# An LSTM step's input and forget gates moved to PSUM, its output gate to an activation of its own, around a re-timed TensorE queue

## The chip, the cores and the metric

The kernel runs on one core of a Trainium2 chip. The metric is the device time of one execution in microseconds. A profile of one further execution is shown beside it; its durations are used for all working.

## The reference

An LSTM over 1024 steps with batch 2 and 256 hidden units is added to its input, and a mixture-of-experts layer over the 2048 resulting tokens is added to that. Cut to what matters:

```
def step(carry, xw_t):
    prev_h, prev_c = carry
    a = xw_t + prev_h @ Wh                      # (2, 1024): i, f, o, g
    i, f, o = sigmoid(a[:, :H]), sigmoid(a[:, H:2*H]), sigmoid(a[:, 2*H:3*H])
    g = tanh(a[:, 3*H:])
    next_c = f * prev_c + i * g
    next_h = o * tanh(next_c)
    return (next_h, next_c), next_h
x = x + lstm(x, cond, Wx, Wh, b)
x = x + moe(x, cond, ...)      # 2 shared experts (silu, 512 wide), 8 routed (gelu, 256 wide), top 2
```

All is float32. The steps of the LSTM depend on each other; the expert layer of a token needs only that token's h.

## The kernel before, in words

The program is one long unrolled stream. `for t in range(T)` walks the 1024 steps. Hidden units lie in K = 2 chunks m of 128. A step goes through these instructions, for m = 0 and then m = 1:

- TensorE (all its instructions are issued by the helper `product`, L255): 32 products `ps<-wh_sb,h`, in the order of `BLOCKS`: three blocks need only chunk 0 of h, then come those that need chunk 1. Float32 makes two passes of each product, so 64 matmuls and 64 weight loads. They add onto the input projections, which small products with `inputs` (`inject`) have put into the bank of these gates before. Chunk m = 0 of the gates is complete after the fifth block.
- VectorE: `transpose(m)` (L787) turns the gates in PSUM so that a gate's values stand beside each other.
- ScalarE: `squash(m)`: one sigmoid of i, o and f together (L790, six values a partition) and one tanh of g (L791), both from PSUM to the SBUF tile `results`.
- VectorE: `forget(m)`, f * c (L794; c is read in PSUM); `cell(m)`: a small copy `seen` (L798), which holds VectorE's queue until g's tanh is there, and a scan of four values (L799), which forms i * g + f * c, writes c to the PSUM bank `cells[m]`, and reads i, g and f * c in SBUF.
- ScalarE: `squash_cell(m)`, tanh(c) (L807), PSUM to PSUM.
- VectorE: `output(m)`, h = o * tanh(c) (L810), into the SBUF tile that the next step's products read.

VectorE's queue order in a step is: transpose 0, transpose 1, forget 0, seen 0, scan 0, forget 1, seen 1, scan 1, output 0, output 1, then at most one or two pieces of filler.

Beside this chain the class `Fill` deals out the rest of the work: input projections for the next 128 steps and the expert layer of a finished group of steps (`GROUPS`), in units, a few after each step: `run_pe` after the 32 products, `run` for ScalarE, `run_dve(0.6)` for VectorE (estimated microseconds that a step may take). `PACES` says in how many steps a group's units have to be spread. A unit that opens one of two PSUM banks waits until VectorE work has let one go. A step without units may get a filler product `busy` with the identity matrix, but only if the first step of its eight had no units either (`spare`). After this come the `inject` products of the next eight steps' bank; their number is chosen with the list `WAITS` so that a boundary of 256 TensorE instructions (`FETCH`) does not fall on the first 16 of the next step's products (`EARLY`). The last group (32 steps) and what is left of the one before it are worked off after the last step (`drain`).

Of the kernel before, what the change touches and what calls it, by code (L numbers as in the profile page):

```python
# [9 lines left out]
F32 = mybir.dt.float32  # L10
BF16 = mybir.dt.bfloat16
AF = mybir.ActivationFunctionType
ALU = mybir.AluOpType
# [3 lines left out]
P = 128  # L17
N = 2
T = 1024
D = 256  # L20
K = D // P
Q = 4
ROWS = P // Q
PAIR = ROWS // 2
TH = PAIR // N
TB = 2 * TH
XB = 128
LOAD = 2
E = 8
# [3 lines left out]
TOP_K = 2  # L33
LAST = 32

GROUPS = [128] * 3 + [32] + [128] * 4 + [64, LAST]

PACES = [128] * 7 + [56, 31, 0]
FILL_BANKS = 2


# [1 line left out]
ROOM = 4  # L43
# [3 lines left out]


FETCH = 256
EARLY = 16  # L50
WAITS = (
    1, 8, 16, 24, 32, 40, 48, 56, 64, 72, 80, 88, 96, 104, 112, 120, 128, 136, 144, 149,
    152, 157, 160, 160, 165, 168, 176, 181, 184, 189, 192, 197, 200, 208, 216, 224, 232,
    240, 248, 256, 264, 272, 280, 288, 296, 304, 312, 320, 328, 336, 344, 352, 360, 368,
    376, 384, 392, 400, 408, 416, 419, 421, 423, 424, 428, 430, 432, 435, 437, 439, 440,
    440, 447, 448, 456, 464, 472, 480, 488, 496, 504, 512, 520, 528, 529, 536, 544, 552,
    560, 568, 576, 584, 592, 600, 608, 616, 624, 632, 640, 648, 656, 664, 672, 680, 688,
    688, 696, 704, 712, 720, 728, 736, 744, 752, 760, 768, 776, 784, 792, 800, 808, 816,
    824, 832, 840, 848, 856, 864, 872, 880, 888, 896, 904, 912, 920, 928, 930, 933, 935,
    936, 940, 942, 944, 947, 949, 951, 952, 956, 958, 960, 963, 965, 968, 976, 984, 992,  # L60
    999, 1000, 1004, 1006, 1008, 1011, 1013,
)
ISSUED = -188
OUT_SCALE = 1.0 / (NS + TOP_K)
# [9 lines left out]
class Fill:  # L74
# [36 lines left out]
    def run(self, queue, budget):  # L111
        while queue and queue[0][0] <= self.step and queue[0][1] <= budget:
            _, cost, fn = queue.popleft()
            budget -= cost
            fn()

    def run_pe(self, count, room):
        done = 0
# [16 lines left out]
def lstm_moe_kernel(  # L135
# [16 lines left out]
    nc = tc.nc  # L152
# [63 lines left out]
    for t0 in range(2 * XB, T, XB):  # L216
        for k in range(K):
            cols = slice(t0, t0 + XB)
# [32 lines left out]
    fill = Fill()  # L251

    def product(*operands, **how):
        fill.issued += 4
        nc.tensor.matmul(*operands, **how)  # L255

    def bank():
        if fill.last:
            pool, name = behind[0]
            behind.rotate(-1)  # L260
        else:
            pool, name = fill_ps, "ps_f"
        return pool.tile([P, 2, 256], F32, name=name)
# [22 lines left out]
    def experts(t0, S):  # L286
# [215 lines left out]
        def last_shared_down(c):  # L502
            if c < 0:
                st["down"] = bank()
                x_kqj = st["down"][:W, 0, :].rearrange("p (q k j) -> p k q j", q=Q, k=K)
                for k in range(K):
                    product(
                        x_kqj[:, k], mov[k], ident_s,
                        start=(k == 0), stop=False, skip_group_check=True,
                    )  # L510
                return
            ps, n = st["down"], NS * HS // P
            for g in range(2):
                product(
                    ps[g * W : (g + 1) * W, 0, :], st["h_s"][:, c + g, :W], w2_sb[:, c + g, :],
                    start=(c + g == 1), stop=(c + 2 == n), skip_group_check=True,
                )
            if c + 2 == n:
                fill.to_dve(0.45, lambda: begin_sum(0, ps), lag=0)
# [11 lines left out]

        def last_add(e2, ps):
            acc = st["acc", 0]
            nc.vector.scalar_tensor_tensor(  # L534
                acc, ps[:, 0, :], st["gates"][:, e2 : e2 + 1], acc, ALU.mult, ALU.add
            )
            fill.let_go()
            if e2 == E // 2 - 1:
                both = bank()[:W, 0, :]
                product(both, fold, acc, start=True, stop=True)  # L540
                total = work.tile([P, D], F32, name="y")[:W]
                nc.scalar.activation(total, both, AF.Copy)  # L542
                nc.sync.dma_start(out=out_tn[t0 : t0 + S], in_=total)

        ups = [
            (int(j == 0), W // P if W > P else 1, lambda b=b, j=j: up(b, j))
# [45 lines left out]
    def h_cols(t):  # L592
        at = EDGE + t % TB * ROWS
        return hs[t // TB % 2][:, :, at : at + N]
# [59 lines left out]
    def inject(banks, grp, i, pieces=1):  # L654
        m, q = divmod(i, Q)
        blk, g = divmod(grp, XB // TH)
        assert all((blk, 4 * m + 2 * (q // 2) + c, g * PAIR) in made for c in range(2))
        for piece in range(pieces):
            w0, w1 = 64 * piece // pieces, 64 * (piece + 1) // pieces
            product(  # L660
                banks[m][0][q * ROWS : (q + 1) * ROWS, w0:w1],
                pairs(blk)[:, 2 * m + q // 2, g].rearrange("p c r -> p (c r)"),
                ident[:, q % 2 * 64 + w0 : q % 2 * 64 + w1],
                start=(piece == 0), stop=False, skip_group_check=True,
            )
# [21 lines left out]

    def results():
        flat = stepsp.tile([P, TB, K, 8 * N], F32, name="results")
        sgm = flat[:, :, :, : 6 * N].rearrange("p u m (a n z) -> p u m a n z", n=N, z=2)
        gf = flat[:, :, :, 6 * N :].rearrange("p u m (n z) -> p u m n z", z=2)
        for m in range(K):
            nc.scalar.activation(sgm[:, :, m, 0, :, 0], zero[:, :, m], AF.Copy)
        return sgm, gf


    nc.scalar.activation(stepp.tile([P, N], F32, name="seen0"), zero[:, 0, 0], AF.Sigmoid)
    nxt_results = results()

    cells = [cells_ps.tile([P, 3, N, 2], F32, name=f"c{m}") for m in range(K)]
    c_prev = [cells[m][:, 1] for m in range(K)]
    for m in range(K):
        nc.vector.memset(cells[m], 0.0)
    nc.vector.tensor_copy(h_cols(0), cond_sb)
# [19 lines left out]
    for t in range(T):  # L728
        fill.step = t
        grp, u = divmod(t, TB)  # L730
        if t % TH == 0:
            cur, nxt = nxt, [gates_tile(m) for m in range(K)]
            ps, turned, busy = [a[0] for a in cur], [a[1] for a in cur], nxt[0][2]
            spare = False
        if u == 0:
            sgm, gf = nxt_results
        if t == 1:
            queue_inputs(0, ROWS)
        if t == XB // 2:
# [15 lines left out]
                    skip_group_check=True,  # L755
                )
        left = max(1, due - t)
        done = fill.run_pe(-(-len(fill.pe) // left), ROOM)
        if t % TH == 0:
            spare = not done  # L760
        if spare and not done:
            product(
                busy, ident, ident.unsqueeze(1).to_broadcast([P, 2, P]),
                start=(t % TH == 0), stop=False, skip_group_check=True,
            )

        if t // TH + 1 < T // TH:
            put = put if t % TH else 0
            fill.issued += WAITS.count(t)

            left = K * Q - put
            count = next(
                (n for n in range(max(0, t % TH + 1 - put), left + 1)
                 if -(fill.issued + 4 * n) % FETCH > EARLY), left)
            first = -(fill.issued + 4 * count) % FETCH
            for i in range(count):
                more = i == count - 1 and first <= EARLY
                inject(nxt, t // TH + 1, put, 2 + first // 4 if more else 1)
                put += 1

        rows = slice(N * (t % TH), N * (t % TH + 1))
        gates = [turned[m].rearrange("p (a r) -> p a r", r=PAIR)[:, :, rows] for m in range(K)]
        c_new = [cells[m][:, t % 2] for m in range(K)]
        seen = [stepp.tile([P, N], F32, name=f"seen{m}") for m in range(K)]

        def transpose(m):
            nc.vector.transpose(turned[m], ps[m])  # L787

        def squash(m):
            nc.scalar.activation(sgm[:, u, m, :, :, 1], gates[m][:, 0:3], AF.Sigmoid)  # L790
            nc.scalar.activation(gf[:, u, m, :, 0], gates[m][:, 3], AF.Tanh)  # L791

        def forget(m):
            nc.vector.tensor_mul(gf[:, u, m, :, 1], sgm[:, u, m, 2, :, 1], c_prev[m][:, :, 1])  # L794

        def cell(m):

            nc.vector.tensor_copy(seen[m], gf[:, u, m, :, 0])  # L798
            nc.vector.tensor_tensor_scan(  # L799
                c_new[m].rearrange("p n z -> p (n z)"),  # L800
                sgm[:, u, m, 0].rearrange("p n z -> p (n z)"),
                gf[:, u, m].rearrange("p n z -> p (n z)"),
                0.0, ALU.mult, ALU.add,
            )

        def squash_cell(m):
            nc.scalar.activation(cells[m][:, 2, :, 0], c_new[m][:, :, 1], AF.Tanh)  # L807

        def output(m):
            nc.vector.tensor_mul(h_cols(t + 1)[:, m], sgm[:, u, m, 1, :, 1], cells[m][:, 2, :, 0])  # L810

        for fn in (transpose, squash):
            for m in range(K):
# [4 lines left out]
            squash_cell(m)  # L818
        for m in range(K):
            output(m)  # L820
        if u == TB // 2 and t + TB < T:
            nxt_results = results()
        else:
            fill.run(fill.act, 1.0)
        c_prev = c_new
        if rest and t % LOAD == 0:
            load_next()
        if t == 2 * TB:
# [3 lines left out]
        if (t + 1) % XB == 0 and t + 1 + XB < T:  # L832
            queue_inputs((t + 1) // XB + 1)
        if u < TB - 1:
            fill.run_dve(0.6)
            continue
        if t < T - 1:
            residual(grp, int(grp == 0 or t - TB in ends), TB)
# [89 lines left out]
```

## Time and profile before

| what | value |
|---|---|
| median of 3 runs | 2257.78 us (2252.64 to 2258.61) |
| the profiled execution | 2256.97 us, of which the span is 2254.8 us |
| busy in the span | PE 2033.5, weight loads 1484.8, DVE 1571.3, ACT 909.5 us |
| mean granted TensorE clock | 0.996 |
| first transposition starts / last pair starts | 10.2 us / 2232.4 us into the span |

The span is the time from the first to the last instruction of the program. Busy time counts the union of an engine's instructions; a group's line gives line, engine, operation, output<-inputs, shape and count, then busy time and mean ns of one, then idle time of the engine just before and what ended it. The `results`, `c` and `ps` of the names stand for all buffers of that name.

### The profile page before, as it was taken

Reading aid. Unit: us, or ns where it says so; the run is one execution under the profiler, and the core shown is the slowest. Engines: PE = TensorE matmul, PEld = TensorE weight load, DVE = VectorE, ACT = ScalarE, POOL = GpSimd, SP = SyncE. Lnnn points to the kernel's source line nnn. Section 1 sums busy time; section 2 is a strip of 40 time slices with the busy share of each in tenths; the row PEclk is TensorE's granted clock in tenths of the full one; section 3 lists DMA queues with packets and bytes.
Section 4 is the critical chain, followed back from the end, with each engine's and each line's share of the span. In section 5 each row is a group of like instructions: output and inputs, shape, how many; then the busy total and the mean of one; then the engine's idle time right before and its main releaser. Section 6 shows DMA issues by size and latency. Waiting matters only on the chain.

```text
span 2254.8 us, 159246 instructions
## 1 busy us (share of the span) xinstructions
PE 2033.5 (90%) x70612; PEld 1484.8 (66%) x70612; DVE 1571.3 (70%) x11041; ACT 909.5 (40%) x6487; POOL 2.7 (0%) x9
## 2 busy tenths in 40 slices
PE   8988899888989889998798899988898988989998
PEld 6666666666666666777666666666666666667787
DVE  5666667776777667777667767676676776667776
ACT  3334344433444334443344443444434344334443
POOL 0000000000000000000000000000000000000000
PEclk9999999999999999999999999999999999999999
DMA  2111100000000000000000000000000000000000
GB/s 65 35 35 35 35 28 5 5 5 7 7 5 5 5 7 7 5 7 7 5 6 5 5 5 7 7 4 5 5 7 7 4 5 5 7 7 5 5 9 7
DMA packets 15330, 23.84 MB, mean 11 GB/s; under 512 B 2864, under 2 KB 14128, under 8 KB 14640
## 3 DMA queue, kind: packets, MB, share of 16 engines
q1 hardware_dynamic: 14352, 12.62, 1.9%
q8 instruction: 552, 9.04, 1.7%
q14 instruction: 138, 1.13, 0.2%
q10 hardware_dynamic: 288, 1.05, 0.1%
HBM read 11.56 MB, written 2.10 MB: 6 GB/s over the span
## 4 chain that ended last, share of the span: by engine, by line
PE 61%; DVE 36%; issue 3%; DMA 0%; SPq 0%; ACT 0%
PE ps L255 53%; DVE ps L787 10%; DVE c L799 10%; PE ps_f L255 8%; DVE results L794 7%; DVE seen L798 6%; DVE h L810 3%; DMA wh_sb<-in_wh_dram 0%; SPq L165 0%; DVE acc L534 0%; SPq L173 0%; SPq L171 0%; SPq L170 0%; DVE acc L492 0%; ACT y L542 0%
## 5 line engine op out<-in xcount | busy, mean ns | idle before, releaser
L255 PE MATMUL ps<-wh_sb,h 128*32 128x64 f32 x65536 | 1143.8, 221 | 214.3 <-DVE h L810 210.5
L255 PEld LDWEIGHTS ps<-wh_sb,h 128*32 128x32 f32 x65536 | 975.1, 110 | 393.1 <-DVE h L810 386.8
L787 DVE STREAM_TRANSPOSE ps<-ps 128x64 f32<-128x64 f32 x2048 | 543.4, 265 | 498.5 <-PE ps L255 426.0
L790 ACT ACTIVATE results<-ps 128x6 f32<-128x6 f32 x2048 | 361.3, 176 | 1103.8 <-DVE ps L787 1009.4
L810 DVE TENSOR_TENSOR h<-results,c 128x2 f32<-128x2 f32 x2048 | 314.2, 153 | 168.4 <-ACT c L807 168.2
L807 ACT ACTIVATE c<-c 128x2 f32<-128x2 f32 x2048 | 321.5, 157 | 217.5 <-DVE c L799 181.7
L799 DVE TENSOR_TENSOR_SCAN c<-results 128x4 f32<-128x4 f32 x2048 | 358.2, 175 | 0.0
L791 ACT ACTIVATE results<-ps 128x2 f32<-128x2 f32 x2048 | 342.4, 167 | 0.0
L798 DVE COPY seen<-results 128x2 f32<-128x2 f32 x2048 | 332.8, 162 | 0.0
L794 DVE TENSOR_TENSOR results<-results,c 128x2 f32<-128x2 f32 x2048 | 319.3, 156 | 0.0
L255 PEld LDWEIGHTS ps<-ident,inputs 128*32 128x32 f32 x2090 | 124.0, 108 | 265.7 <-issue 228.4
L255 PE MATMUL ps<-ident,inputs 128*32 128x64 f32 (+2 forms) x2090 | 263.9, 230 | 0.3
L255 PE MATMUL ps_f<-x2T,w_sb 128*128 128x256 f32 (+3 forms) x640 | 173.4, 379 | 0.0
L255 PE MATMUL ps_f<-x2T,r_sb 128*128 128x256 f32 (+3 forms) x640 | 173.2, 378 | 0.0
L255 PE MATMUL ps_f<-r_sb,h_r 128*128 128x256 f32 (+1 forms) x520 | 165.9, 419 | 0.9 <-DVE acc L492 0.9
L255 PEld LDWEIGHTS ps_f<-x2T,r_sb 128*128 128x128 f32 (+1 forms) x640 | 88.5, 184 | 22.8
L255 PEld LDWEIGHTS ps_f<-x2T,w_sb 128*128 128x128 f32 (+1 forms) x640 | 86.7, 184 | 21.8 <-issue 0.2
L255 PEld LDWEIGHTS ps_f<-r_sb,h_r 128*128 128x128 f32 (+1 forms) x520 | 80.0, 184 | 23.3 <-DVE acc L492 1.3
L255 PE MATMUL ps_f<-xT_sb,wx_sb 128*128 128x256 f32 (+2 forms) x384 | 84.5, 346 | 0.3 <-ACT inputs L613 0.3
L255 PE MATMUL ps<-ident 128*128 128x256 f32 x232 | 82.8, 443 | 1.4 <-POOL ident masks.py:199 1.4
L255 PE MATMUL ps_f<-w_sb,h_s 128*128 128x256 f32 (+1 forms) x256 | 82.6, 419 | 0.0
L492 DVE SCALAR_TENSOR_TENSOR acc<-ps_f,gate,acc 128x256 f32<-128x256 f32 (+1 forms) x128 | 61.1, 478 | 1.2 <-PE ps_f L255 1.0
(87 smaller groups left out, 475.1 us busy)
## 6 DMA issues: line engine op xcount, KB each, us to landing
r_sb<-in_r_w1T_dram SPq DMA_DIRECT2D x16, 128.0 KB, 2.5
r_sb<-in_r_w2T_dram SPq DMA_DIRECT2D x16, 128.0 KB, 2.1
out_dram<-acc SPq DMA_DIRECT2D x15, 128.0 KB, 2.1
xT_sb<-in_xT_dram SPq DMA_DIRECT2D x14, 128.0 KB, 2.5
wx_sb<-in_wx_dram ACTq DMA_DIRECT2D x2, 512.0 KB, 4.3
wh_sb<-in_wh_dram SPq DMA_DIRECT2D x2, 512.0 KB, 6.2
w_sb<-in_s_w1T_dram SPq DMA_DIRECT2D x8, 128.0 KB, 2.2
w_sb<-in_s_w3T_dram SPq DMA_DIRECT2D x8, 128.0 KB, 2.2
```

Of the source, the lines that this page charges most:

```text
L255: nc.tensor.matmul(*operands, **how)
L492: nc.vector.scalar_tensor_tensor(acc, ps, st["gate"][:, i, e : e + 1], acc, ALU.mult, ALU.add)
L787: nc.vector.transpose(turned[m], ps[m])
L790: nc.scalar.activation(sgm[:, u, m, :, :, 1], gates[m][:, 0:3], AF.Sigmoid)
L791: nc.scalar.activation(gf[:, u, m, :, 0], gates[m][:, 3], AF.Tanh)
L794: nc.vector.tensor_mul(gf[:, u, m, :, 1], sgm[:, u, m, 2, :, 1], c_prev[m][:, :, 1])
L798: nc.vector.tensor_copy(seen[m], gf[:, u, m, :, 0])
L799: nc.vector.tensor_tensor_scan(c_new[m].rearrange("p n z -> p (n z)"), sgm[:, u, m, 0].rearrange("p n z -> p (n z)"), gf[:, u, m].rearrang ...
L807: nc.scalar.activation(cells[m][:, 2, :, 0], c_new[m][:, :, 1], AF.Tanh)
L810: nc.vector.tensor_mul(h_cols(t + 1)[:, m], sgm[:, u, m, 1, :, 1], cells[m][:, 2, :, 0])
```

## The change

Four things change together.

1. The step's cell. The sigmoid takes i and f alone (four values) and writes them to `cells[m]`, the PSUM bank that holds c; o's sigmoid becomes an activation of its own, put ahead of tanh(c) in ScalarE's queue, and goes to SBUF. The scan reads i in PSUM. f * c reads f in PSUM and c in a copy in SBUF, which a new `tensor_copy` makes behind each `output(m)`. The small instruction `seen` becomes a product that reads the PSUM bank and g. The zeroing activations of `results()` go.
2. The TensorE queue. The order after the 32 products becomes: a product that opens the bank of eight steps (always on their first step, 32 columns wide if units follow, 2 x 128 columns otherwise), injections, units, and the filler product in every step that has neither units nor that opening product. The rule for the number of injections counts what follows them (`then`), has new limits, and a new list `WAITS`.
3. The groups: steps 800 to 927 become two groups of 64, `PACES` are set anew, and `run_dve` gets 0.55 in place of 0.6.
4. The end: the last sum and its way out are cut into two halves of 128 columns.

```diff
-GROUPS = [128] * 3 + [32] + [128] * 4 + [64, LAST]
-PACES = [128] * 7 + [56, 31, 0]
+GROUPS = [128] * 3 + [32] + [128] * 3 + [64] * 3 + [LAST]
+PACES = [128] * 6 + [60, 60, 48, 27, 0]
...
-EARLY = 16
+EARLY = 12
...
         def last_add(e2, ps):
             acc = st["acc", 0]
-            nc.vector.scalar_tensor_tensor(
-                acc, ps[:, 0, :], st["gates"][:, e2 : e2 + 1], acc, ALU.mult, ALU.add
-            )
+            if e2 < E // 2 - 1:
+                cols = [slice(0, D)]
+            else:
+                cols = [slice(0, P), slice(P, D)]
+                total = work.tile([P, D], F32, name="y")[:W]
+            for i, c in enumerate(cols):
+                nc.vector.scalar_tensor_tensor(
+                    acc[:, c], ps[:, 0, c], st["gates"][:, e2 : e2 + 1], acc[:, c],
+                    ALU.mult, ALU.add,
+                )
+                if len(cols) > 1:
+                    both = bank()[:W, 0, :P]
+                    product(both, fold, acc[:, c], start=True, stop=True)
+                    nc.scalar.activation(total[:, c], both, AF.Copy)
+                    nc.sync.dma_start(out=out_tn[t0 : t0 + S][:, :, c], in_=total[:, c])
...
     def results():
-        flat = stepsp.tile([P, TB, K, 8 * N], F32, name="results")
-        sgm = flat[:, :, :, : 6 * N].rearrange("p u m (a n z) -> p u m a n z", n=N, z=2)
-        gf = flat[:, :, :, 6 * N :].rearrange("p u m (n z) -> p u m n z", z=2)
-        for m in range(K):
-            nc.scalar.activation(sgm[:, :, m, 0, :, 0], zero[:, :, m], AF.Copy)
-        return sgm, gf
+        flat = stepsp.tile([P, TB, K, 4, N], F32, name="results")
+        gf = flat[:, :, :, :2].rearrange("p u m a n -> p u m (a n)")
+        return gf.rearrange("p u m (n z) -> p u m n z", z=2), flat[:, :, :, 2], flat[:, :, :, 3]
...
-    cells = [cells_ps.tile([P, 3, N, 2], F32, name=f"c{m}") for m in range(K)]
-    c_prev = [cells[m][:, 1] for m in range(K)]
+    cells = [cells_ps.tile([P, 5, N, 2], F32, name=f"c{m}") for m in range(K)]
+    c_prev = [zero[:, 0, m] for m in range(K)]
...
-        done = fill.run_pe(-(-len(fill.pe) // left), ROOM)
-        if t % TH == 0:
-            spare = not done
-        if spare and not done:
+        count = -(-len(fill.pe) // left)
+        done = fill.ready_pe(count, ROOM)
+        opens = t % TH == 0
+        if opens:
+            wide = busy[:, :1, :ROWS] if done else busy
             product(
-                busy, ident, ident.unsqueeze(1).to_broadcast([P, 2, P]),
-                start=(t % TH == 0), stop=False, skip_group_check=True,
-            )
+                wide, ident, ident[:, : wide.shape[2]].unsqueeze(1).to_broadcast(wide.shape),
+                start=True, stop=False, skip_group_check=True,
+            )
+            put = 0
+        then = 4 * (done or not opens) + WAITS.count(t)
+        early = EARLY + (8 if t >= T - LAST else 0)
...
+            first = [-(fill.issued + 4 * n + then) % FETCH for n in ways]
+            n = next((n for n, f in zip(ways, first) if early < f < FETCH - 2), ways[-1])
...
+        fill.run_pe(count, ROOM)
+        if not (done or opens):
+            product(
+                busy, ident, ident.unsqueeze(1).to_broadcast(busy.shape),
+                start=False, stop=False, skip_group_check=True,
+            )
...
         def squash(m):
-            nc.scalar.activation(sgm[:, u, m, :, :, 1], gates[m][:, 0:3], AF.Sigmoid)
+            nc.scalar.activation(cells[m][:, 3:5, :, 1], gates[m][:, 0:3:2], AF.Sigmoid)
             nc.scalar.activation(gf[:, u, m, :, 0], gates[m][:, 3], AF.Tanh)
 
         def forget(m):
-            nc.vector.tensor_mul(gf[:, u, m, :, 1], sgm[:, u, m, 2, :, 1], c_prev[m][:, :, 1])
+            nc.vector.tensor_mul(gf[:, u, m, :, 1], cells[m][:, 4, :, 1], c_prev[m])
 
         def cell(m):
-            nc.vector.tensor_copy(seen[m], gf[:, u, m, :, 0])
+            nc.vector.tensor_mul(
+                stepp.tile([P, 2, N], F32, name=f"seen{m}"), cells[m][:, 3:5, :, 1],
+                gf[:, u, m, :, 0].unsqueeze(1).to_broadcast([P, 2, N]),
+            )
             nc.vector.tensor_tensor_scan(
                 c_new[m].rearrange("p n z -> p (n z)"),
-                sgm[:, u, m, 0].rearrange("p n z -> p (n z)"),
+                cells[m][:, 3].rearrange("p n z -> p (n z)"),
                 gf[:, u, m].rearrange("p n z -> p (n z)"),
                 0.0, ALU.mult, ALU.add,
             )
 
         def squash_cell(m):
+            nc.scalar.activation(out_gate[:, u, m], gates[m][:, 1], AF.Sigmoid)
             nc.scalar.activation(cells[m][:, 2, :, 0], c_new[m][:, :, 1], AF.Tanh)
 
         def output(m):
-            nc.vector.tensor_mul(h_cols(t + 1)[:, m], sgm[:, u, m, 1, :, 1], cells[m][:, 2, :, 0])
+            nc.vector.tensor_mul(h_cols(t + 1)[:, m], out_gate[:, u, m], cells[m][:, 2, :, 0])
...
             output(m)
+            nc.vector.tensor_copy(c_kept[:, u, m], c_new[m][:, :, 1])
...
-        c_prev = c_new
+        c_prev = [c_kept[:, u, m] for m in range(K)]
...
-            fill.run_dve(0.6)
+            fill.run_dve(0.55)
```

## The prediction

> **What bounds the kernel now.** I read the page first: the chain that ended last is TensorE and VectorE in turn, and its lines are those of one LSTM step, so the time is 1024 steps one after another.
>
> ```profile
> PE 61%; DVE 36%; issue 3%; DMA 0%; SPq 0%; ACT 0%
> ...
> L255 PE MATMUL ps<-wh_sb,h 128*32 128x64 f32 x65536 | 1143.8, 221 | 214.3 <-DVE h L810 210.5
> ...
> L787 DVE STREAM_TRANSPOSE ps<-ps 128x64 f32<-128x64 f32 x2048 | 543.4, 265 | 498.5 <-PE ps L255 426.0
> L790 ACT ACTIVATE results<-ps 128x6 f32<-128x6 f32 x2048 | 361.3, 176 | 1103.8 <-DVE ps L787 1009.4
> L810 DVE TENSOR_TENSOR h<-results,c 128x2 f32<-128x2 f32 x2048 | 314.2, 153 | 168.4 <-ACT c L807 168.2
> L807 ACT ACTIVATE c<-c 128x2 f32<-128x2 f32 x2048 | 321.5, 157 | 217.5 <-DVE c L799 181.7
> L799 DVE TENSOR_TENSOR_SCAN c<-results 128x4 f32<-128x4 f32 x2048 | 358.2, 175 | 0.0
> L791 ACT ACTIVATE results<-ps 128x2 f32<-128x2 f32 x2048 | 342.4, 167 | 0.0
> L798 DVE COPY seen<-results 128x2 f32<-128x2 f32 x2048 | 332.8, 162 | 0.0
> L794 DVE TENSOR_TENSOR results<-results,c 128x2 f32<-128x2 f32 x2048 | 319.3, 156 | 0.0
> ```
>
> Then the timeline of an undisturbed step (start, length, engine, line):
>
> ```profile
> 230.19 0.60 DVE L787 STREAM_TRANSPOSE ps<-ps 128x64 f32<-128x64 f32 x2 [0.57 <-PE ps L255]
> ...
> 230.49 0.18 ACT L790 ACTIVATE results<-ps 128x6 f32<-128x6 f32 x1 [1.05 <-DVE ps L787]
> ...
> 230.70 0.15 DVE L794 TENSOR_TENSOR results<-results,c 128x2 f32<-128x2 f32 x1
> ...
> 230.82 0.18 ACT L790 ACTIVATE results<-ps 128x6 f32<-128x6 f32 x1
> ...
> 231.03 0.16 DVE L794 TENSOR_TENSOR results<-results,c 128x2 f32<-128x2 f32 x1
> ...
> 231.22 0.17 DVE L799 TENSOR_TENSOR_SCAN c<-results 128x4 f32<-128x4 f32 x1
> 231.30 0.15 DVE L810 TENSOR_TENSOR h<-results,c 128x2 f32<-128x2 f32 x1
> ```
>
> From the same records in ns, the first transposition at 0, the critical loop runs through chunk 1: transposition 336-601, sigmoid 634-811, f*c 843-999, scan starts 1034, and chunk 0's h starts at 1116, 82 behind it (the scan holds VectorE's issue), ends 1267; products from 1319, last one's start at 2203, next transposition of chunk 1 at 2491. Chunk 0's own path (f*c starts 510, scan 699-874, tanh 908-1065) would let h start at 1099: 17 ns of slack. Its f*c cannot start before 510 even with an earlier sigmoid: chunk 1's transposition holds the queue 174 ns, as steps where that one is late show (972 after 798).
>
> Third, the starts of all first transpositions. The median distance is 2.154 us. The span is 10.2 (head) + 1023 x 2.154 = 2203.5 + 18.7 (longer steps) + 22.4 (tail). I sorted the 18.7 by what the timeline shows in each longer step:
>
> - 5.4: TensorE clock. A step or a few with no units and no filler, then slow products (steps 13-16: 3.2; 672-673 and 801-802: 2.2):
>
> ```profile
> 40.00:44.00 4.00, 2.97 (x116) 2.73 (x113) 1.47 (x12) 0.79 (x6) 0.00 (x0) 0.51 0.02 1
> ...
> 1466.00:1470.00 4.00, 2.84 (x136) 2.41 (x124) 2.77 (x22) 2.02 (x14) 0.00 (x0) 1.00 0.01 4
> 1470.00:1474.00 4.00, 3.93 (x128) 3.74 (x132) 1.52 (x12) 0.94 (x7) 0.00 (x0) 0.57 0.02 4
> ```
>
> - 8.3: some 35 steps in which the last products of the step come late with no wait that the profile shows. They sit at every 256th TensorE instruction, 2.3-2.9 us after the start of a packet of the instruction queue:
>
> ```profile
> 375.31 0.27 DVE L787 STREAM_TRANSPOSE ps<-ps 128x64 f32<-128x64 f32 x1 [0.23 <-PE ps L255]
> ...
> 375.76 0.31 PE L255 MATMUL ps<-wh_sb,h 128*32 128x64 f32 x4 [0.20 <-issue]
> ```
>
> - 5.0: TensorE full. With two units of 256 columns and an injection a step takes 2.174 us on average (105 such steps).
>
> **The change part by part.** Sum against the profiled execution: 2256.97 = span 2254.8 + 2.2; the median is 0.8 above it.
>
> *The sigmoid.* L790 (six values, PSUM to SBUF) takes 176 ns, L791 (two, same route) 167, L807 (two, PSUM to PSUM) 157. So PSUM as target is 10 cheaper, four values cost 2 to 5 more than two: 159-162, 14-17 saved. On chunk 1 all of it is on the loop; chunk 0 is held at 1099, so no more than 17 can come. I take 15: 2.139 a clean step. No row shows this exact form; bounds are 5 (only fewer values) and 17.
>
> *Reading PSUM on VectorE.* The scan now reads i in PSUM, and f*c has PSUM and SBUF swapped. Rows: L794 and L810, with one PSUM operand, take 156 and 153, the SBUF copy L798 162; so no surcharge, perhaps 5 less. [...] By the rows it is 0. [...]
>
> *o's sigmoid.* Two more activations a step, 167 each. The first is issued about 72 behind tanh(g) of chunk 1 (705), at some 777, and tanh(c) may start at 908: hidden with 60 to spare. The second starts about 975, tanh(c) of chunk 1 not before 1226. Without this cover each would cost about 70 (issue distance of L790 to L791). TensorE's first product into chunk 1's bank now waits for this later read (ends about 1140); that product comes after 1500. The zeroing activations that go (22 us busy) were off the path.
>
> *The c copies and `seen`.* Two more VectorE instructions a step, 74 of issue each. One lies between the two h products (1116 and 1432), one before the filler; VectorE waits 498.5 us for the transpositions, and one filler piece of 0.48 from 1.57 us ends before 2.139. `seen` reads PSUM too; the scan is held by f*c, not by it (tanh(g) ends 872, `seen` needs about 905, the scan starts at 1018). Cost 0; uncovered, 74 a step.
>
> *TensorE's queue.* The programs show each step's TensorE work in order. Now every step has units or filler, so the clock steps should go: -5.2. [...] Row 1466-1470 has TensorE 2.84 of 4 us busy, and the fall follows one thin step. [...] I follow the row.
>
> *Instruction boundaries.* A late boundary costs when the one before it lay in the last instructions ahead of a step's products: they were injections behind the units, issued at some 870 ns, and a fetch then took 2.9-3.9 us where 3.4 were left. There are 78 such pairs after, 73 before, but these instructions are now injections and units issued at 100-300: about 4.0 us are left. I keep 1.0 of 8.3: -7.3. Bounds 0 and -8.3.
>
> *Full steps.* From rows: 256-column product 0.53, 128-column 0.30, injection 0.03, 32-column opening product 0.22 (products of eight columns start 0.11 apart, two passes). This puts 141 steps of before over 2.154 and gives 6.1 where 4.9 was measured; after, 174 steps and 11.5, scaled 9.3: +4.4. About 17 of these steps carry the opening product; in the others it lies in TensorE's slack. So the 15 ns count in about 848 steps: -12.7.
>
> *The tail.* With 0.55 for VectorE the pieces for routing go one or two a step and the sums queue up: four units and five sums followed the last step, now eight and eight. Four units last 1.99 us in the tail, and the first must wait for one more sum of 0.52: +2.5. Halving the last sum and copy: (0.48+0.65+0.38) becomes about 1.3, but two stores at 0.55 of issue: -0.2. Moved queues: SP issues one store more here, nothing else; POOL nothing.
>
> Sum: -12.7 + 4.4 - 5.2 - 7.3 + 2.3 = -18.5: span 2236.3, profiled 2238.5, as a median 2239.
>
> **The rivals.** *A (0.82): as summed*, 2228 to 2250; the unknowns are the saving (5 to 17: +8.5 to -1.7), the boundaries (+7.3, -1) and the full steps (some 4 either way).
>
> *B (0.08): PSUM reads cost VectorE.* [...] It ends slower than before from some 23 ns more on the scan: 17 of slack on chunk 0, and 6 a step for the -5.8. [...] Against: 156 and 153 beside 162.
>
> *C (0.07): only the queue's part works.* The strided write into the bank makes the sigmoid no faster, or chunk 0 turns out to hold at 1116: -5.8 is left, 2252; with the boundaries kept 2259.
>
> *D (0.03): the change does not do what it says.* o's sigmoid delays tanh(c): past 908 it would cost each step up to 70 ns, +60 us. The issue distances speak against it.
>
> **How the numbers follow.** Less than 0.3% (6.8 us, 2251.0 to 2264.6) cannot be told from no change. Faster: A, 0.82, and a little of C: 0.83. Same: most of C, 0.06. Slower: B and D, 0.11. The range of eight in ten is A with C's better half, 2228 to 2255.
>
> **What would show it.** Right: the sigmoid's row near 160 ns at four values, the scan at 170-175, the median step at 2.139; no clock row below 0.9 after the start; few issue waits ahead of `ps<-wh_sb,h`; the tail near 24.7 us. Wrong: a scan or f*c above 190; tanh(c) starting more than 40 behind its scan; a step of 2.154 with a shorter sigmoid, which would mean that chunk 0 decides; full steps costing more than 14.

## The result: 3.3% slower, and the profile after

The changed kernel takes 2331.9 us (median of 4 runs, 2330.1 to 2332.7), the kernel before 2256.8 (4 runs, 2252.6 to 2258.6): ratio 1.033, 95% interval 1.032 to 1.035. That is 75 us slower, where 18 us faster was predicted. The profiled execution has a span of 2328.1 us against 2254.8.

First the page of the changed kernel: the chain of work that ended last by engine, and the rows that answer to those shown of before (busy us and mean ns of one, then the idle time ahead of them and who ended it).

```profile
PE 63%; DVE 34%; issue 3%; DMA 0%; SPq 0%; ACT 0%
...
L267 PE MATMUL ps<-wh_sb,h 128*32 128x64 f32 x65536 | 1131.4, 221 | 298.6 <-DVE results L846 294.6
...
L810 ACT ACTIVATE c<-ps 128x4 f32<-128x4 f32 x2048 | 323.6, 158 | 1118.1 <-DVE ps L807 1019.1
L823 DVE TENSOR_TENSOR_SCAN c<-c,results 128x4 f32<-128x4 f32 x2048 | 355.9, 174 | 70.8
...
L819 DVE TENSOR_TENSOR seen<-c,results 128x4 f32<-128x4 f32 x2048 | 324.3, 158 | 0.0
...
L814 DVE TENSOR_TENSOR results<-c,results 128x2 f32<-128x2 f32 x2046 | 300.0, 147 | 0.0
```

Of the instructions on the loop none became longer: the sigmoid takes 158 ns (176 before), f*c 147 (156), the scan 174 (175), `seen` 158 (162). So no operation became dear. What is new stands in the last column: VectorE is idle for 70.8 us ahead of the scan, where the row of before had 0.0. TensorE's wait for its products grew from 214 to 299 us. The page puts that wait down to the copy of c (L846), which is wrong: the first product starts at 1387 ns, 55 behind the end of h (1332) and 5 before that copy ends (1392). Before, the distance behind h was 54 (1321 behind 1267). TensorE still waits for h.

The timeline of an undisturbed step (start, length, engine, line) shows where h is late. First `seen` and the scan of chunk 1 in the kernel before, where the scan starts while `seen` is still running (it lasts until 231.26):

```profile
231.10 0.16 DVE L798 COPY seen<-results 128x2 f32<-128x2 f32 x1
231.22 0.17 DVE L799 TENSOR_TENSOR_SCAN c<-results 128x4 f32<-128x4 f32 x1
```

Then the step of the changed kernel:

```profile
233.54 0.60 DVE L807 STREAM_TRANSPOSE ps<-ps 128x64 f32<-128x64 f32 x2 [0.50 <-PE ps L267]
...
234.05 0.14 DVE L814 TENSOR_TENSOR results<-c,results 128x2 f32<-128x2 f32 x1
234.11 0.16 DVE L819 TENSOR_TENSOR seen<-c,results 128x4 f32<-128x4 f32 x1
...
234.30 0.17 DVE L823 TENSOR_TENSOR_SCAN c<-c,results 128x4 f32<-128x4 f32 x1
234.39 0.15 DVE L814 TENSOR_TENSOR results<-c,results 128x2 f32<-128x2 f32 x1
234.45 0.15 DVE L819 TENSOR_TENSOR seen<-c,results 128x4 f32<-128x4 f32 x1
...
234.64 0.17 DVE L823 TENSOR_TENSOR_SCAN c<-c,results 128x4 f32<-128x4 f32 x1
234.72 0.15 DVE L835 TENSOR_TENSOR h<-results,c 128x2 f32<-128x2 f32 x1
```

From the same records in ns behind the first transposition (step 100 here and in all kernels below), chunk 0 then chunk 1:

| | f*c ends | `seen` ends | scan starts | chunk 0's h starts | median step |
|---|---|---|---|---|---|
| before | 665, 999 | 743, 1078 | 699, 1034 | 1116 | 2.154 us |
| after | 652, 1000 | 733, 1065 | 767, 1099 | 1181 | 2.221 us |

Before, the scan starts 34 ns behind the end of f*c, while `seen` is still running. After, it starts 34 behind the end of `seen`. The built program says the same: each instruction in it carries the semaphore and the value that it waits for, and the scan's value on VectorE's own semaphore points to the instruction two ahead of it (f*c) in the kernel before, to the one directly ahead (`seen`) in the changed kernel. The new `seen` reads the tile `cells[m]` in PSUM, which the scan writes; the old one read only SBUF. The scan is 65 late, h is 65 late, and 1023 steps of 0.067 us make some 68 of the 73 us that the span grew by.

Sorted in one way for every kernel, the spans are made of (us): head, 1023 median steps, what longer steps add, tail. A longer step counts as clock if its products ran slower, as boundary if its last products came late with no wait shown, else as full. (The prediction's own sort of before, 5.4, 8.3 and 5.0, differs from this one by up to 0.6.)

| kernel (one profiled execution each) | median step | clock | boundary | full | tail |
|---|---|---|---|---|---|
| before | 2.154 | 5.5 | 8.6 | 4.4 | 22.4 |
| after | 2.221 | 2.1 | 2.7 | 14.8 | 26.5 |
| e1 new queue, `seen` in SBUF | 2.188 | 3.3 | 4.0 | 23.9 | 24.8 |
| e2 before, `seen` reads the scan's bank | 2.224 | 8.1 | 0.9 | 0.7 | 22.4 |
| e3 new queue, old cell | 2.155 | 1.2 | 2.5 | 27.5 | 24.7 |
| e4 old queue, new cell, `seen` in SBUF | 2.188 | 8.4 | 7.5 | 6.5 | 22.4 |
| e5 old queue, repaired cell | 2.142 | 0.0 | 6.8 | 7.1 | 22.4 |
| e6 new queue, repaired cell | 2.142 | 1.0 | 2.8 | 31.2 | 24.7 |
| e7 new queue, old cell, no opening product | 2.155 | 0.0 | 1.9 | 10.4 | 26.3 |
| e8 repaired cell, no opening product, old groups | 2.142 | 1.0 | 1.2 | 13.9 | 22.3 |
| e9 before, `seen` reads another bank | 2.154 | 4.4 | 4.2 | 11.5 | 22.4 |

### The profile page after: what moved, and what is told of

It is laid out like the page before. It is cut to its first block, busy times and chain, and to the rows that moved or that the text cites. A ratio compares the mean times of both kernels' runs of the same rounds, so it can differ in the third digit from the quotient of the medians.

```text
span 2328.1 us, 164128 instructions
## 1 busy us (share of the span) xinstructions
PE 2014.5 (87%) x71052; PEld 1522.7 (65%) x71052; DVE 1701.0 (73%) x13115; ACT 1039.3 (45%) x8409; POOL 2.7 (0%) x9
## 4 chain that ended last, share of the span: by engine, by line
PE 63%; DVE 34%; issue 3%; DMA 0%; SPq 0%; ACT 0%
PE ps L267 53%; DVE c L823 12%; PE ps_f L267 10%; DVE ps L807 9%; DVE seen L819 6%; DVE results L814 4%; DVE results L846 2%; DVE h L835 2%; DMA wh_sb<-in_wh_dram 0%; DVE acc L504 0%; SPq L177 0%; SPq L185 0%; SPq L183 0%; SPq L182 0%; DVE acc L552 0%
## 5 line engine op out<-in xcount | busy, mean ns | idle before, releaser
L267 PE MATMUL ps<-wh_sb,h 128*32 128x64 f32 x65536 | 1131.4, 221 | 298.6 <-DVE results L846 294.6
L810 ACT ACTIVATE c<-ps 128x4 f32<-128x4 f32 x2048 | 323.6, 158 | 1118.1 <-DVE ps L807 1019.1
L823 DVE TENSOR_TENSOR_SCAN c<-c,results 128x4 f32<-128x4 f32 x2048 | 355.9, 174 | 70.8
L831 ACT ACTIVATE results<-ps 128x2 f32<-128x2 f32 x2048 | 356.3, 174 | 0.0
L811 ACT ACTIVATE results<-ps 128x2 f32<-128x2 f32 x2048 | 343.7, 168 | 0.0
L819 DVE TENSOR_TENSOR seen<-c,results 128x4 f32<-128x4 f32 x2048 | 324.3, 158 | 0.0
L846 DVE COPY results<-c 128x2 f32<-128x2 f32 x2048 | 309.4, 151 | 0.0
L814 DVE TENSOR_TENSOR results<-c,results 128x2 f32<-128x2 f32 x2046 | 300.0, 147 | 0.0
L267 PEld LDWEIGHTS ps<-ident,inputs 128*32 128x32 f32 x2108 | 151.9, 110 | 20.2 <-issue 14.8
L267 PE MATMUL ps<-ident 128*128 128x256 f32 (+1 forms) x524 | 152.3, 374 | 1.7 <-POOL ident masks.py:199 1.4
L267 PEld LDWEIGHTS ps_f<-x2T,w_sb 128*128 128x128 f32 (+1 forms) x704 | 94.1, 184 | 22.3 <-PE ps L267 0.5
L267 PEld LDWEIGHTS ps<-ident 128*128 128x128 f32 x524 | 79.4, 190 | 25.7 <-POOL ident masks.py:199 1.4
```

Source lines behind the costliest of these rows:

```text
L810: nc.scalar.activation(cells[m][:, 3:5, :, 1], gates[m][:, 0:3:2], AF.Sigmoid)
L814: nc.vector.tensor_mul(gf[:, u, m, :, 1], cells[m][:, 4, :, 1], c_prev[m])
L819: nc.vector.tensor_mul(stepp.tile([P, 2, N], F32, name=f"seen{m}"), cells[m][:, 3:5, :, 1], gf[:, u, m, :, 0].unsqueeze(1).to_broadcast([P ...
L823: nc.vector.tensor_tensor_scan(c_new[m].rearrange("p n z -> p (n z)"), cells[m][:, 3].rearrange("p n z -> p (n z)"), gf[:, u, m].rearrange ...
L831: nc.scalar.activation(out_gate[:, u, m], gates[m][:, 1], AF.Sigmoid)
L846: nc.vector.tensor_copy(c_kept[:, u, m], c_new[m][:, :, 1])
```

## The experiments

All ran beside the kernel before, whose median was 2250.6, 2250.7 and 2250.4 us in the three batches (e1 to e4, e5 to e8, e9); ratios are to it. That is 6 us below the 2256.8 above, and the mean granted clock of these 36 runs is 0.9986, where the profiled execution of before, which the table shows, had 0.996. Where a kernel mixes parts, its list `WAITS` was brought as near as it would go to the wait instructions of its own program, as the originals' lists are; so the places of the injections differ a little between such kernels. "Queue" is short for the order of TensorE's work with its filler, the groups of tokens and the tail.

**e1: the changed kernel, `seen` from SBUF again**

```diff
-            nc.vector.tensor_mul(
-                stepp.tile([P, 2, N], F32, name=f"seen{m}"), cells[m][:, 3:5, :, 1],
-                gf[:, u, m, :, 0].unsqueeze(1).to_broadcast([P, 2, N]),
-            )
+            nc.vector.tensor_copy(
+                stepp.tile([P, N], F32, name=f"seen{m}"), gf[:, u, m, :, 0]
+            )
```

> The changed kernel, with one instruction put back: `seen` is again a copy of tanh(g) from SBUF to SBUF and reads nothing of the bank of `cells`. Theory W (the scan now waits for the end of `seen`, because `seen` reads the bank that the scan writes; 34 ns after its end the scan starts): the scan is released by f*c again, chunk 0's at about 687 and chunk 1's at about 1001 ns of the step, in place of 767 and 1099; chunk 0's h starts 82 behind, at about 1083, against 1181 in the changed kernel and 1116 in the kernel before. The median step falls from 2.221 to about 2.12 us, and the time to 2240 us (2230 to 2250), below the kernel before. Rival X (reading and writing PSUM from VectorE and ScalarE, the two more activations or the two more copies of c cost the time): they all stay, so the step stays at 2.21 to 2.22 and the time at about 2325 to 2332.

Measured: 2305.2 us, ratio 1.024 (1.023 to 1.026), step 2.188. Neither forecast. The scans are released by f*c again, as theory W said: they start at 686 and 1018 (687 and 1001 expected). And yet two thirds of the gain are missing (33 ns of a step gained, where 101 were expected). The timeline, from chunk 0's scan on:

```profile
232.50 0.17 DVE L822 TENSOR_TENSOR_SCAN c<-c,results 128x4 f32<-128x4 f32 x1
...
232.57 0.18 ACT L830 ACTIVATE results<-ps 128x2 f32<-128x2 f32 x1
...
232.76 0.16 ACT L831 ACTIVATE c<-c 128x2 f32<-128x2 f32 x1
232.83 0.17 DVE L822 TENSOR_TENSOR_SCAN c<-c,results 128x4 f32<-128x4 f32 x1
...
232.95 0.16 DVE L834 TENSOR_TENSOR h<-results,c 128x2 f32<-128x2 f32 x1
```

tanh(c) (L831) starts at 953, 93 behind the end of its scan (860); in the changed kernel that distance is 34. For chunk 1 it is 94. So h starts at 1142, held by tanh(c), not at 1100. All instructions of the line of tanh(c), in e1:

```profile
L831 ACTq EVENT_SEMAPHORE  x2048: 17/17/17, 11.4 to 2280.8; - x187
L831 ACT ACTIVATE c<-c x2048: 157/157/183, 11.5 to 2280.9; 128x2 f32<-128x2 f32 x187
```

and in the changed kernel:

```profile
L832 ACT ACTIVATE c<-c x2048: 157/157/157, 11.2 to 2302.9; 128x2 f32<-128x2 f32 x187
```

In e1 every tanh(c) has got a wait instruction of its own ahead of it. In the program that one waits for the scan, and tanh(c) itself for ScalarE's own sigmoid of i and f, which had written the same bank 0.49 us before (it ends some 460 ns into the step, tanh(c) starts at 953). The price is 59 ns (93 - 34). Taking the wait away at the scan brought out another one behind it.

**e2: the kernel before, `seen` alone changed**

```diff
-            nc.vector.tensor_copy(seen[m], gf[:, u, m, :, 0])
+            nc.vector.tensor_mul(seen[m], c_prev[m][:, :, 1], gf[:, u, m, :, 0])
```

> The kernel before, with one part of the change alone: `seen` becomes a product of tanh(g) with the old c, so that it reads the PSUM bank of `cells` which the scan writes; nobody reads its result, as before. Theory W: the scan starts 34 ns after the end of `seen`, chunk 0's h at about 1174 in place of 1116, the step is 2.154 + 0.058 = 2.21 us and the time about 2257 + 59 = 2316 us (2305 to 2325), though a product of two values takes no longer than the copy did. Rival X: nothing that X names is added, the time stays at 2257.

Measured: 2317.0 us, ratio 1.029 (1.027 to 1.031). One instruction, no longer than the copy it replaces (153 ns), costs 66 us:

```profile
235.49 0.15 DVE L798 TENSOR_TENSOR seen<-c,results 128x2 f32<-128x2 f32 x1
...
235.68 0.17 DVE L799 TENSOR_TENSOR_SCAN c<-results 128x4 f32<-128x4 f32 x1
235.76 0.15 DVE L810 TENSOR_TENSOR h<-results,c 128x2 f32<-128x2 f32 x1
```

`seen` of chunk 1 ends at 1067, the scan starts at 1101, h at 1185. The step is 0.070 longer. 1023 of these would be 72; in the profiled executions the full and boundary steps give some of it back (13.0 before, 1.6 here), because a longer step hides them.

**e9: the same product, reading a bank that the scan does not write**

```diff
-            nc.vector.tensor_copy(seen[m], gf[:, u, m, :, 0])
+            nc.vector.tensor_mul(seen[m], gates[m][:, 3], gf[:, u, m, :, 0])
```

> The kernel before, with `seen` as a product again, as in e2, but its PSUM operand is the gate g in the bank of the gates, which the scan does not touch. It separates the read from the wait in e2 (2317 us, step 2.224). In the built program the scan waits for f*c as in the kernel before; new is a wait instruction ahead of chunk 0's `seen`, for the second transposition (it ends at about 600 ns, so that `seen` starts at about 640 in place of 573, and chunk 0's scan some 15 late, within the 17 of slack of chunk 0). Theory W (only the wait counts): the scan of chunk 1 starts at about 1034 and the step stays at 2.15 to 2.16 us, the time at 2251 to 2262. Rival R (a `seen` that reads PSUM is itself what costs): the step is 2.22 as in e2, the time about 2317.

Measured: 2258.7 us, ratio 1.003 (1.002 to 1.004), step 2.154.

```profile
230.65 0.15 DVE L790 TENSOR_TENSOR seen<-ps,results 128x2 f32<-128x2 f32 x1
230.76 0.17 DVE L791 TENSOR_TENSOR_SCAN c<-results 128x4 f32<-128x4 f32 x1
230.85 0.15 DVE L802 TENSOR_TENSOR h<-results,c 128x2 f32<-128x2 f32 x1
```

`seen` runs from 918 to 1071, the scan starts at 1034 beside it. Same instruction, same kind of operand, another bank: nothing lost in the step. e2's cost is the wait, not the read. The wait instruction ahead of chunk 0's `seen` is there as expected (21 ns, from 522), but in the program it is for the first transposition, which had ended at 266; so `seen` starts at 588, not at 640 (582 before). (The 0.3% come from longer steps, whose order of injections was planned anew for fewer waits on TensorE.)

**e3 and e4: the two halves of the change apart**

```diff
 # e3: new queue, old cell (results(), squash, forget, cell, squash_cell, output of before)
-            nc.scalar.activation(cells[m][:, 3:5, :, 1], gates[m][:, 0:3:2], AF.Sigmoid)
+            nc.scalar.activation(sgm[:, u, m, :, :, 1], gates[m][:, 0:3], AF.Sigmoid)
...
 # e4: the reverse, on the kernel before, with `seen` as in e1
```

> The changed kernel's order of TensorE's work, groups and tail, with the step's VectorE and ScalarE work of the kernel before. The prediction's steps for this part were +4.4 full, -5.2 clock, -7.3 boundaries, +2.3 tail: 2251 us at a step of 2.154. From the changed kernel's trace I now read a clock share of 2.1 (5.5 before), late boundaries of 2.7 (8.6 before), a tail of 26.5 (22.4 before), but 16 steps with the opening product and two units of 256 columns that last 0.44 longer, some +7: about 2255, no difference that shows. A rival, that this part carries the loss: 2300 or more.

Measured: 2272.8 us, ratio 1.010 (1.008 to 1.011). The queue's part alone costs 22 us. Against the profiled execution of before its clock, boundary and tail terms came out near the prediction (-4.3, -6.1 and +2.3, by the table); its full steps add 27.5 where before had 4.4. That makes 15 us between these two spans; the other 6 or 7 are that the kernel before ran faster here than when it was profiled. The expectation missed as well: it had read the full steps in the changed kernel, where each step is 0.067 longer and only +10 of the +23 show.

> The new cell (sigmoid of i and f to the bank, o's sigmoid by itself, copies of c) with `seen` as an SBUF copy, and the order of TensorE's work, groups and tail of the kernel before. Theory W: the step falls by what the sigmoid (18 ns) and f*c (13 ns) lost in length, from 2.154 to about 2.123, in some 880 of the steps: 2257 - 27 = 2230 us. The prediction's own reckoning, 15 ns of the sigmoid alone in 848 steps, gives 2244. Rival X: above 2300.

Measured: 2289.6 us, ratio 1.017 (1.016 to 1.019), step 2.188: the wait ahead of tanh(c) is there as in e1. The forecasts of 2230 and 2244 missed for that; rival X (above 2300) missed too.

**e5 and e6: f*c reads both gates**

```diff
-            nc.vector.tensor_mul(gf[:, u, m, :, 1], cells[m][:, 4, :, 1], c_prev[m])
+            nc.vector.tensor_mul(
+                cf[:, u, m], cells[m][:, 3:5, :, 1],
+                c_prev[m].unsqueeze(1).to_broadcast([P, 2, N]),
+            )
```

`cf` are the places of f*c and of the later copy of c; the products of i with c in the second are overwritten. `seen` is e1's copy.

> As e4 (new cell, `seen` from SBUF, the old order of TensorE's work), and f*c multiplies both sigmoids of the bank with c in one instruction of four values; the two products of i with c go where the copy of c is written later and are never read. Theory V: in e1 and e4 the new bank wait had come back in front of tanh(c), as a separate wait instruction on ScalarE for its own sigmoid, because no VectorE instruction ahead of the scan had read both gates in the bank; with f*c reading both, that instruction is gone from the program, tanh(c) of chunk 0 starts 34 behind its scan's end (about 897 ns, 953 in e1), chunk 0's h 82 behind the second scan (about 1100), and the step falls from 2.188 to about 2.145 us: 2289.6 - 41 = 2248 us (2243 to 2256). Rival Y: o's sigmoid, which stands between tanh(g) and tanh(c) on ScalarE, is what holds tanh(c): it stays where it is, the step stays at 2.188 and the time at 2285 to 2295.

Measured: 2239.6 us, ratio 0.9955 (0.9943 to 0.9968), step 2.142. The time is 3 us below theory V's range, which counted from e4; e4's runs had a mean granted clock of 0.996, those of e5 0.999. The wait instruction is gone from the program:

```profile
226.88 0.17 DVE L800 TENSOR_TENSOR_SCAN c<-c,results 128x4 f32<-128x4 f32 x1
...
226.95 0.18 ACT L808 ACTIVATE results<-ps 128x2 f32<-128x2 f32 x1
...
227.09 0.16 ACT L809 ACTIVATE c<-c 128x2 f32<-128x2 f32 x1
...
227.22 0.17 DVE L800 TENSOR_TENSOR_SCAN c<-c,results 128x4 f32<-128x4 f32 x1
227.30 0.15 DVE L812 TENSOR_TENSOR h<-results,c 128x2 f32<-128x2 f32 x1
```

The scan ends at 863, tanh(c) starts at 896, with o's sigmoid where it was; h starts at 1102, 81 behind the second scan. Rival Y is out, and so is the last of X: two more activations and two more copies a step are all in this kernel, which is 0.45% faster than the kernel before: little, but clear of its interval. It is the fastest kernel here.

> As e1 (the changed kernel with `seen` from SBUF), and f*c over both gates as in e5. Theory V: the step falls from 2.188 to about 2.145, the time from 2305 to 2264 us (2258 to 2272): the cell as it was meant, with the queue part's loss of some 20 us still in it. Rival Y: 2300 to 2308.

Measured: 2263.4 us, ratio 1.006 (1.004 to 1.007), step 2.142. With e1 this is the sum for the cell, as ratios to the kernel before: 1.033 for the changed kernel, 1.024 with the scan's wait gone, 1.006 with the one ahead of tanh(c) gone too.

**e7 and e8: without the opening product**

```diff
-        if opens:
-            wide = busy[:, :1, :ROWS] if done else busy
+        if opens and not done:
             product(
-                wide, ident, ident[:, : wide.shape[2]].unsqueeze(1).to_broadcast(wide.shape),
+                busy, ident, ident.unsqueeze(1).to_broadcast(busy.shape),
...
 # e8 also: GROUPS, PACES and run_dve(0.6) of before
```

> As e3 (the old cell, the new order of TensorE's work), without the 32-column opening product in those groups of eight steps whose first step has units; fillers write only the rows of the bank that an injection has opened. Theory O (the opening product ahead of injections and units delays the units by 0.48 us, not by the 0.22 of the prediction): the 14 steps with two units lose 0.50 each, 61 with one unit 0.073 each, a few others 0.5: 2272.8 - 14 = 2259 us (2254 to 2263). Rival Q (injections ahead of the units are what costs, as in the 114 steps with two units and one injection that last 0.036 longer): above 2267.

Measured: 2256.4 us, ratio 1.003 (1.002 to 1.004): 16 us less than e3, full steps 10.4 in place of 27.5. TensorE's rows of a step of e3 with the opening product (`ps<-ident`, 32 columns), an injection and two units, and of one without it:

```profile
287.98 0.41 PE L265 MATMUL ps<-ident 128*128 128x32 f32 x2
288.32 0.30 PE L265 MATMUL ps<-ident,inputs 128*32 128x64 f32 x2
288.55 1.13 PE L265 MATMUL ps_f<-xT_sb,wx_sb 128*128 128x256 f32 x4
289.61 0.70 PE L265 MATMUL ps<-wh_sb,h 128*32 128x64 f32 x35
```

```profile
297.12 0.28 PE L265 MATMUL ps<-ident,inputs 128*32 128x64 f32 x2
297.32 1.13 PE L265 MATMUL ps_f<-xT_sb,wx_sb 128*128 128x256 f32 x4
298.38 0.82 PE L265 MATMUL ps<-wh_sb,h 128*32 128x64 f32 x44
```

The steps begin at 287.78 and 297.03. The units start 765 ns into the first and 289 into the second: 476 later for one product of 32 columns. Why it costs so much is not shown.

> As e6, without the opening product, and with the groups of tokens, their paces and VectorE's 0.6 us budget of the kernel before. If V and O hold: 10.3 head + 1023 x 2.145 + some 12 of longer steps + 22.4 tail + 2.2 = 2241 us (2236 to 2250), below the kernel before by 0.2 to 0.6%. If the gain of the cell is eaten by full steps, as those of e3 were: 2250 or more.

Measured: 2242.8 us, ratio 0.9968 (0.9956 to 0.9979): as forecast, and faster than before, but not than e5. Its boundaries cost 1.2 (6.8 in e5), its full steps 13.9 (7.1). So the new order of TensorE's work brings no gain in any run here, even without the opening product: e7 is 6 us above the kernel before, e8 3 us above e5.

## Why the prediction was wrong, step by step

The forecast of the span, -18.5 us, missed the measured +73.3 by 92. Of these, 81 lie in the median step (+68.5 where -12.7 was forecast), 6 in the full steps, and less than 2 each in clock, boundaries and tail.

- **`seen`, priced at 0: this is the step that failed.** The text saw that `seen` now reads PSUM, and argued from times alone: f*c ends last, so f*c holds the scan. That holds only for the waits of the kernel before. `seen` ends later than f*c in both kernels (1078 against 999 before); nobody had to wait for that end, until the change made it share the scan's bank. Price: 65 ns a step, shown by e2 (step +0.070), e9 (+0) and the program's wait values. The prediction had bounded an uncovered `seen` by 74 for its issue; the bound for its end, from 1000 to 1065, was never drawn, nor the rival that it makes.
- **The sigmoid, 15 ns on chunk 1.** Its length fell by 18 (176 to 158). In e5 and e6, where nothing else holds the scan, the step fell by 12: sigmoid 19 earlier (792 against 811), but chunk 1's f*c takes 162 where the old one took 156 (159 in e1 with two values, so it is not the four). The term was right in size. In the changed kernel none of it arrives.
- **PSUM reads on VectorE, 0.** Right: f*c 147 against 156, scan 174 against 175. No run shows a surcharge for these reads: rival B needed some 23 ns more on the scan, and the scan took 1 less. The kernel ended slower, as B said, but B's cause is absent.
- **o's sigmoid, hidden.** Right: tanh(c) starts 33 behind its scan in e5, 34 in the changed kernel.
- **Copies of c, 0.** Right, by e5: with them in it the step is 2.142, 0.012 below before.
- **Clock, -5.2.** Not shown as a gain. In the profiled executions the clock share was 5.5, 8.1, 8.4, 4.4 and 0.0 with the old order and 2.1, 3.3, 1.2, 1.0, 0.0 and 1.0 with the new. But the kernel before had a mean granted clock of 0.9986 over its 36 runs beside the experiments, the kernels with the new order 0.9987 over their 32 (the changed kernel alone 0.997). Other kernels with the old order lie on both sides: e2, e4 and e9 at 0.996 to 0.997, e5 at 0.999. The 5.4 that the prediction meant to remove were those of one execution. With the old order the clock fell at steps 13, 672 and 801 in the kernel before, at 501, 544, 800 and 917 in e4, and nowhere between the first and the last step in e5. What sets the falls off is not shown. In the changed kernel they follow steps that have units, but of 8 or 64 columns, so that no filler is sent (steps 396 and 500). Around the first one TensorE was busy for 3.05 of 4 us (PE busy is the second figure, the granted clock the third from the end):

```profile
892.00:896.00 4.00, 3.05 (x106) 2.77 (x110) 2.63 (x23) 1.77 (x16) 0.00 (x0) 0.90 0.00 0
896.00:900.00 4.00, 4.00 (x123) 3.15 (x116) 2.15 (x17) 1.20 (x11) 0.00 (x0) 0.67 0.02 6
```

- **Boundaries, -7.3.** Near in e3, -6.1 against the profiled execution of before. The -5.9 of the changed kernel do not count for it: e2, with the old order and an equally long step, has 0.9 us of late boundaries, so a longer step alone hides them.
- **Full steps, +4.4.** Wrong by a factor of five: +23 in e3, +10 in the changed kernel, where the longer step hides the rest. The mis-sized term is the opening product: 0.22 was taken from the pace of short products; ahead of an injection and units it delays them by 0.48, so the 14 steps with two units last 0.50 longer, and the 61 with one unit, put down as slack, last 0.073 longer. e7 gives 17 of it back.
- **Tail, +2.3.** Right in e1, e3 and e6 (24.7 to 24.8 against 22.4); 26.5 in the changed kernel and 26.3 in e7. What makes these 1.7 more was not pursued.

Had `seen` been left in SBUF and nothing else, the forecast would still have been wrong: e1 shows the second wait, e3 the full steps. That e5 runs at 2239.6, the number predicted, is chance: it has the old queue, and the kernel before beside it ran at 2250.7, so that it gains 11 us and not 18.

What stays open is the rule by which the layer that sets the waits decides that tanh(c) needs a wait for ScalarE's own sigmoid. All that the runs show is that the wait is absent where an instruction on VectorE behind that sigmoid and ahead of tanh(c) reads both gates in the bank (the changed kernel, e5, e6, e8), and present where none does (e1, e4).

## What to carry to other kernels

When a change moves a tile into a PSUM bank, list for that bank every instruction that reads or writes it on any engine, and price a wait for the end of each one ahead of the next writer, also on one engine and also for instructions whose result nobody reads (here the scan starts 34 ns behind the end of `seen`, 65 late). Read the waits with their values in the built program before the times: the name of the semaphore was the same in both kernels, and only the value moved from f*c to `seen`. When a wait is taken away, look whether the same order comes back as a wait instruction elsewhere.

## What the hardware showed beside that

- A small filler instruction ahead of an injection and units cost more than twice the 0.22 us reckoned for it: one of 32 columns, with a 128x128 weight tile where the injections have 128x32, put the units 476 ns later (e3).
- A longer step pays part of its own cost: boundary and full steps shrink from 13.0 to 1.6 us when the step is 0.070 longer (e2), and the same full steps grow from 14.8 to 27.5 and 31.2 us when the step goes from 2.221 to 2.155 and 2.142 (e3, e6). An excess read at one step length must not be carried to another.
- A wait instruction by itself lasts 17 ns in its row, yet tanh(c) behind it starts 59 later (e1).
